# A three-part feed-forward/attention block in fp32: bursts of row maxima kept single, turned tiles in two banks, first loads on two queues

## The chip, the cores and the metric

One NeuronCore of a Trainium2 chip runs the whole kernel. The metric is the device time of one execution in microseconds (us); the median of three executions is compared. Besides those times there is one profiled execution, whose trace gives each instruction's start and length on each engine: TensorE (PE, with its weight loads PEld), VectorE (DVE), ScalarE (ACT), GpSimd (POOL), and SyncE (SP), which issues most DMAs.

## The reference

The input x has 4 sequences of 1024 tokens with 256 features, all in fp32. Three steps are added to it in turn: half a gated feed-forward layer of its layer norm, causal attention of its layer norm (16 heads of 16 features, with a rotation of q and k), and the same half feed-forward layer again.

```python
x = x + 0.5 * ffn(layernorm(x))          # silu(g) * u, 704 hidden
x = x + attn(layernorm(x))               # causal softmax, 16 heads of 16
x = x + 0.5 * ffn(layernorm(x))
# ffn:  g = (x @ gate_w.T) * gate_s ; u = (x @ up_w.T) * up_s
#       out = ((silu(g) * u) @ down_w.T) * down_s
# attn: att = softmax(q k^T / 4 + mask) ; out = (att v) @ Wo.T
```

## The kernel before

**Tiling.** The 4096 tokens are cut into eight blocks of 512, two to a sequence. For each block the kernel runs a first feed-forward layer (`ffn(i, 1)`), the projections (`qkv`), the attention, and a second feed-forward layer (`ffn(i, 2)`). Tokens of a block lie in four tiles of 128.

**Norm and turning.** `norm` makes statistics (VectorE, L364 and L367), a power on GpSimd (L373, L374) and the scaled tile (L386 on ScalarE, L382 on VectorE). The normed tile must have features on partitions. For most blocks that is done by VectorE's 32x32 transposes (L423) and a round trip through DRAM (`spread`, L433 and L439). For the first block's first layer, the first block's projections and the last block's second layer there is `turned` instead: four TensorE transposes of two tiles into one PSUM bank, and two copies out of it, one by ScalarE and one by VectorE (L456). In the very first layer, products of the identity with itself (`idle`, L411) stand ahead of the turns and ahead of the first gate product.

**Feed-forward.** Eleven products of 512 columns, two instructions each (L510), go into PSUM banks; ScalarE takes tanh (L524, L544), VectorE makes the gated hidden tile hT (L547, L550, and L527, L530 for the half chunk), and four down products of six instructions each (L570) are added to x (L576).

**Attention.** Each batch of two head groups is handled in two passes over scores. The first pass computes scores by query (L783), VectorE adds the causal mask where needed (L808) and takes negated row maxima (L835, L818) into nm. TensorE turns nm (L863), ScalarE copies it out (L868), and DMAs write it as an additional row into qT (L873), so that the second pass's scores by key (L898) already have the maximum taken off. ScalarE takes exp of these (L907), GpSimd masks the diagonal (L919), and products with v (L943) follow. A "half" is one pair of heads of one unit of scores: it takes two banks. A burst is two halves at a time, each using two of the four row groups of the array, so four banks: two halves of maxima, two of exps, or one of each.

**What sets the order.** All work is put into one program order by `Planner`, which runs when the program is built, with costs written by hand. `burst()` says which two halves could go next (a half of maxima with one of exps where both can, otherwise two alike). `step` compares that burst with the best other operation. After a burst it waits for `GAP` (1.6 us of other TensorE work) before the next one, except that a second burst may follow at once while TensorE is in "row" mode and fewer than `VISIT` (2) have been made: that is the variable `more`. PSUM has eight banks: bursts take from all of them; other products ("d") have at most four at a time.

**Start.** `load_first` issues the four tiles of block 0's x on SP (L353). `consts` issues the small gus table on ScalarE's queue, then the weights on SP, builds identity and causal mask on GpSimd, and there scales gus (L309, L310), which tanh and hidden use. The x of block 1 (L344) is issued after them, then the projections' weights.

Of the kernel before, what the change touches and what calls it, by code (L numbers as in the profile page):

```python
# [17 lines left out]
P = 128  # L18
# [25 lines left out]
class Planner:  # L44
# [83 lines left out]

    def step(self, burst):
        b = burst()  # L130
        more = self.mode == "row" and self.visit < self.VISIT
        due = b is not None and (more or self.since >= self.GAP)
        best = None
        for eng in self.ENGINES:
            for c in self.candidates(eng):
                s = max(c[0], self.busy["pe"] + 0.05) if eng == "pe" else c[0]
                if c[2].mode == "col" and self.mode == "full" and self.busy["pe"] < self.ready(c[2]) + self.PATIENCE:
                    s += self.HOLD
                if eng == "pe" and due and any(k.slot is None and k.kind == "d" for k in c[2].takes):
                    s += self.DUE  # L140
                key = (s, c[1])
                if best is None or key < best[0]:
                    best = (key, c)
        if b is not None:
            pe = self.busy["pe"]
            at = max(b[0], pe)
            if more:
                wait = self.SECOND
            else:
                wait = self.WAIT[self.mode]  # L150
                if self.since < self.GAP:
                    at += self.GAP - self.since
                elif self.since < self.LONG and b[2] is not None:
                    at = max(at, b[2] - 0.853 - 0.2 - self.SECOND)
            key = (max(at, pe + 0.05) - wait, 0)
            if best is None or key < best[0]:
                halves = b[1]
                us = max(h.us for h in halves) + 0.03 + (0.0 if self.mode == "row" else self.CHANGE["row"])
                at = max(b[0], pe, at if self.since >= self.GAP else 0.0)
                for h in halves:  # L160
                    h.us = us
                    self.place(h, at)
                self.visit = self.visit + 1 if self.mode == "row" else 1
                self.mode, self.since = "row", 0.0
                return b
        assert best is not None, "nothing can be placed"
        (s, _), (at, _, op, q) = best
        if op.eng == "pe":
            self.since += op.us
            if op.mode != self.mode:  # L170
                op.us += self.CHANGE[op.mode]
                self.mode = op.mode
        self.place(op, at)
        if q is not None:
            q.popleft()
        else:
            self.loose[op.eng].remove(op)
        return None
# [6 lines left out]
def dve_us(n):  # L185
    return n / 960 + 0.07


def act_us(n, ptr=0):
    return n / 1200 + 0.09 + 0.09 * ptr  # L190
# [3 lines left out]
def tile_macaron(  # L194
# [12 lines left out]
    nc = tc.nc  # L207
    B, T, D = x.shape
    I = wd.shape[0]
    H, HD, HP = 16, 16, 32  # L210
# [4 lines left out]
    BLK = 512  # L215
# [3 lines left out]
    NC = D // P  # L219
# [12 lines left out]
        xn=(4, [P, D]),  # L232
        xq=(2, [P, D]),
        xnT=(2, [P, NC, BLK]),
# [16 lines left out]
    for kind, (n, _) in shapes.items():  # L251
# [10 lines left out]
    ident = cpool.tile([P, P], F32, name="ident")  # L262
# [9 lines left out]
    plan = Planner(  # L272
        {k: v[0] for k, v in shapes.items()} | {k: len(v) for k, v in lasting.items()} | dict(d=dense, score=8),
        dict(d="bank", score="bank"),
    )
# [10 lines left out]
    xf_ = x.rearrange("b (k n p) d -> (b k) p n d", p=P, n=NB)  # L286
# [10 lines left out]
    def consts():  # L297
        nc.scalar.dma_start(out=gus_sb, in_=gus)
        w = wgu.rearrange("(c p) i -> p c i", p=P)
        for a, e in cuts:  # L300
            nc.sync.dma_start(out=wgu_sb[:, :, a:e], in_=w[:, :, a:e])
        nc.sync.dma_start(out=ds_sb, in_=ds.partition_broadcast(P))
        nc.sync.dma_start(out=wd_sb[:, :NF, :], in_=wd[: NF * P].rearrange("(c p) d -> p c d", p=P))
        nc.sync.dma_start(out=wd_sb[HALF:, NF, :], in_=wd[NF * P :])
        nc.gpsimd.memset(mhalf, -0.5)
        make_identity(nc, ident)
        make_causal_mask(nc, causal, mask_val=MASKED)

        nc.gpsimd.tensor_scalar(gus_sb[:, 0, :], gus_sb[:, 0, :], 0.5, None, ALU.mult)  # L309
        nc.gpsimd.tensor_tensor(gus_sb[:, 1, :], gus_sb[:, 1, :], gus_sb[:, 0, :], ALU.mult)  # L310

# [19 lines left out]
    filled = {k: [] for k in lasting}  # L331
# [2 lines left out]
    gu_loaded = Op("dma", 0.0, lambda: None)  # L334
    wd_loaded = Op("dma", 0.0, lambda: None)
    gu_loaded.done, wd_loaded.done = 7.5, 16.0
    wd_scaled = [Op("dve", 0.35, partial(scaled_wd, c), [wd_loaded], prio=4) for c in range(NI)]

    xb = [Buf("x") for _ in range(NBLK)]
    x0, x1, x2 = {}, {}, {}  # L340
# [9 lines left out]

    def load_first(j):
        def emit():
            nc.sync.dma_start(out=xb[0].tile[:, j, :], in_=xf_[0][:, j, :])  # L353

        x0[0, j] = Op("dma", 0.45, emit, takes=[xb[0]], tail=3.2)
        return x0[0, j]


# [49 lines left out]
    def idle(d, n):  # L408

        for _ in range(n):  # L410
            nc.tensor.matmul(d.tile[:, :P], ident, ident, start=True, stop=True)  # L411
# [31 lines left out]

    def turned(pair, j, xnT, prio, later, idles=0):

        d = Buf("d")

        def emit():
            idle(d, idles)
            for n, (xn, _) in enumerate(pair):  # L450
                for c in range(NC):
                    o = (c * 2 + n) * P
                    nc.tensor.transpose(d.tile[:, o : o + P], xn.tile[:, ts(c, P)], ident)

        def copy(c):
            (nc.vector.tensor_copy if c else nc.scalar.copy)(  # L456
                by_tile(xnT.tile[:, c])[:, j - 1 : j + 1],
                d.tile[:, ts(c, 2 * P)].rearrange("p (j a t) -> p j a t", j=2, t=HP),
            )

        t = Op("pe", 4 * 0.107, emit, [p[1] for p in pair], [d, xnT], [p[0] for p in pair], prio=prio)
        k = [Op("act", act_us(D), partial(copy, 0), [t], uses=[d, xnT], prio=later)]
        return t, [*k, Op("dve", dve_us(D), partial(copy, 1), [t], uses=[d, xnT], prio=later)]


    def ffn(i, which):
# [5 lines left out]
        xnT, xs = Buf("xnT"), Buf("xs")  # L472
        by_dma = (i, which) not in ((0, 1), (NBLK - 1, 2))
        very_first = (i, which) == (0, 1)
# [3 lines left out]
        for j in range(0, NB, 2):  # L478
            first, rest, pair = norm(i, j, src, 4, "xn")
# [17 lines left out]
            loose += squared + moves  # L497
        if very_first:

            for o in (f for k in filled.values() for f in k):  # L500
                o.deps += copies
        mids = []

        def product(d, cols, takes):
            for k in range(NC):

                def emit(k=k):
                    if very_first and cols.stop == 2 * I and not k:
                        idle(d, 2)
                    nc.tensor.matmul(  # L510
                        d.tile, wgu_sb[:, k, cols], by_tile(xnT.tile[:, k]), start=(k == 0), stop=(k == NC - 1)
                    )

                need = [*copies, gu_loaded]
                o = Op("pe", mm_us(BLK), emit, need, [] if k else takes, [d, xnT] if k else [xnT], prio=3)
                mids.append(o)
            return o
# [3 lines left out]
        d, a = Buf("d"), Buf("ta")  # L521
# [10 lines left out]
            )  # L532

        g = product(d, slice(2 * NF * P, 2 * I), [d, a, hT[NF]])
        t = Op("act", act_us(BLK, 1), tanh, [g], uses=[d, a], prio=2)
        v = Op("dve", dve_us(BLK), gated, [t], uses=[d, a], prio=2)
        h = Op("dve", dve_us(BLK), hidden, [v, *filled["hL"]], uses=[d, a, hT[NF]], prio=2)
        loose += [t, v, h]
# [233 lines left out]
    def max_half(blk, unit, pair, nm, reduces):  # L772
# [69 lines left out]

        for e in range(2):
            head(e)
        first.pair = pair
        return first

    def row_of_max(blk, g, nm, reduces):
# [38 lines left out]
    def exp_half(blk, unit, pair, pT, masks):  # L887
# [41 lines left out]
                last.append(Op("pool", 0.45, mask, done, uses=[pT], prio=0))  # L929
                loose_att.append(last[-1])  # L930
        masks.extend(last)
        first.pair = pair
        return first

    def weigh(blk, g, us, units, pTs, masks, av):
# [192 lines left out]
    with tc.manual_schedule():  # L1128
        for op in firsts:
            plan.place(op, plan.busy["dma"])  # L1130
        consts()
        plan.busy.update(dict.fromkeys(plan.busy, 3.5))
        plan.busy.update(act=5.0, dma=9.0)
        plan.place(loads.popleft(), 9.0)
        later()
        plan.busy.update(dma=20.0)
        plan.add(*wd_scaled, *(o for f in filled.values() for o in f))
        while True:
            next_ffn()
            pending = maxes or exps or todo  # L1140
            if not pending and not any(plan.loose.values()) and not any(any(q.values()) for q in plan.queues.values()):
                break
            b = plan.step(burst)
            if b is not None:
                for h in b[1]:
                    (maxes if maxes and h is maxes[0] else exps).popleft()
# [65 lines left out]
```

## Time and profile before

| | |
|---|---|
| median of 3 executions | 1060.93 us (1059.57 to 1061.2) |
| profiled execution | 1061.41 us, span of its instructions 1059.5 us |
| mean granted TensorE clock | 0.998 |
| TensorE busy | 1045.2 us (99%), 6546 records |
| VectorE busy | 807.8 us (76%) |
| ScalarE busy | 431.3 us (41%) |
| GpSimd busy | 295.0 us (28%) |
| DMA | 40.38 MB, mean 38 GB/s |

The span runs from the first to the last instruction; the execution's time has a little around it. In the timelines below, the columns are the start and the length in us, engine, line, operation, what it writes and reads, and how many records are merged; in brackets stand the idle time before it and what ended that. In windows, the columns are the stretch, its length, busy time (and records) of PE, PEld, DVE, ACT and POOL, the granted clock, the DMA share and GB/s. Matmul records overlap in the pipeline, so starts are a better measure than lengths.

### The profile page before, as it was taken

Reading aid. Unit: us, or ns where it says so; the run is one execution under the profiler, and the core shown is the slowest. Engines: PE = TensorE matmul, PEld = TensorE weight load, DVE = VectorE, ACT = ScalarE, POOL = GpSimd, SP = SyncE. Lnnn points to the kernel's source line nnn. Section 1 sums busy time; section 2 is a strip of 40 time slices with the busy share of each in tenths; the row PEclk is TensorE's granted clock in tenths of the full one; section 3 lists DMA queues with packets and bytes.
Section 4 is the critical chain, followed back from the end, with each engine's and each line's share of the span. In section 5 each row is a group of like instructions: output and inputs, shape, how many; then the busy total and the mean of one; then the engine's idle time right before and its main releaser. Section 6 shows DMA issues by size and latency. Waiting matters only on the chain.

```text
span 1059.5 us, 17448 instructions
## 1 busy us (share of the span) xinstructions
PE 1045.2 (99%) x6546; PEld 535.3 (51%) x6546; DVE 807.8 (76%) x1874; ACT 431.3 (41%) x821; POOL 295.0 (28%) x503
## 2 busy tenths in 40 slices
PE   8999999999999999999999999999999999999998
PEld 5645555454454464454544554463635644535465
DVE  6678989878898598778787898678798887783342
ACT  3213444345424444435343454444353454354421
POOL 5222431423111744212114432421215321122200
PEclk9999999999999999999999999999999999999999
DMA  8210210210202102100110102101021010010000
GB/s 288 57 41 2 71 31 7 65 31 4 71 8 61 41 2 51 32 30 31 51 51 11 31 13 59 31 22 40 2 61 41 11 51 2 11 51 12 11 20 20
DMA packets 43139, 40.38 MB, mean 38 GB/s; under 512 B 3952, under 2 KB 35760, under 8 KB 42928
## 3 DMA queue, kind: packets, MB, share of 16 engines
q1 hardware_dynamic: 42912, 39.27, 13.7%
q8 instruction: 51, 0.84, 0.3%
q14 instruction: 32, 0.26, 0.1%
q10 hardware_dynamic: 144, 0.01, 0.0%
HBM read 19.60 MB, written 15.20 MB: 33 GB/s over the span
## 4 chain that ended last, share of the span: by engine, by line
PE 90%; DVE 7%; DMA 1%; issue 1%; ACT 1%; SPq 1%; POOL 0%; DVEq 0%; ACTq 0%; POOLq 0%
PE bank L510 26%; PE bank L783 16%; PE bank L570 16%; PE bank L943 12%; PE bank L898 9%; PE bank L643 5%; PE bank L682 3%; PE bank L1015 2%; DVE nm L835 2%; DVE bank L808 1%; DMA x<-in_x 1%; DVE nm L818 1%; DVE hT L550 1%; DVE xs L423 0%; PE bank L863 0%
## 5 line engine op out<-in xcount | busy, mean ns | idle before, releaser
L907 ACT ACTIVATE pT<-bank 128x512 f32<-128x512 f32 x576 | 298.4, 601 | 305.3 <-PE bank L898 304.8
L835 DVE TENSOR_REDUCE nm<-bank 128x1 f32<-128x512 f32 (+2 forms) x640 | 330.6, 575 | 18.2 <-PE bank L898 17.0
L510 PE MATMUL bank<-xnT,wgu_sb 128*128 128x512 f32 x704 | 322.0, 601 | 1.6 <-DVE nm L835 0.7
L898 PE MATMUL bank<-qT,kT 17*128 17x512 f32 (+3 forms) x1536 | 287.0, 515 | 0.0
L783 PE MATMUL bank<-kT,qT 16*128 16x512 f32 (+3 forms) x1536 | 284.3, 508 | 2.5 <-DVE hT L550 1.7
L510 PEld LDWEIGHTS bank<-xnT,wgu_sb 128*128 128x128 f32 x704 | 127.0, 190 | 168.1 <-issue 112.5
L919 POOL TENSOR_SCALAR_AFFINE_SELECT pT<-pT 128x256 f32<-128x256 f32 x256 | 99.2, 407 | 393.6 <-ACT pT L907 393.4
L783 PEld LDWEIGHTS bank<-kT,qT 16*128 16x128 f32 x1536 | 110.8, 184 | 133.2 <-issue 35.9
L570 PE MATMUL bank<-wd_sb,hT 128*128 128x256 f32 x640 | 151.1, 382 | 1.1 <-DVE hT L550 1.1
L943 PE MATMUL bank<-pT,va 128*32 128x512 f32 (+3 forms) x1536 | 137.1, 490 | 1.4 <-DVE nm L835 1.3
L570 PEld LDWEIGHTS bank<-wd_sb,hT 128*128 128x128 f32 x640 | 122.2, 192 | 19.6 <-issue 1.5
L808 DVE TENSOR_TENSOR bank<-bank,causal 128x256 f32<-128x256 f32 (+1 forms) x320 | 104.2, 372 | 33.1 <-PE bank L898 28.8
L898 PEld LDWEIGHTS bank<-qT,kT 17*128 17x128 f32 x1536 | 109.7, 184 | 10.4 <-issue 3.6
L544 ACT ACTIVATE ta<-bank,gus_sb 128x512 f32<-128x512 f32 x80 | 54.9, 686 | 124.7 <-PE bank L510 124.4
L943 PEld LDWEIGHTS bank<-pT,va 128*32 128x32 f32 x1536 | 44.3, 109 | 96.4 <-issue 65.1
L547 DVE SCALAR_TENSOR_TENSOR ta<-ta,bank 128x512 f32<-128x512 f32 x80 | 54.8, 685 | 47.3 <-ACT ta L544 46.6
L975 POOL TENSOR_TENSOR oq<-oq 128x512 f32<-128x512 f32 x32 | 40.5, 1267 | 113.8 <-DVE oq L972 93.9
L550 DVE SCALAR_TENSOR_TENSOR hT<-bank,gus_sb,ta 128x512 f32<-128x512 f32 x80 | 59.5, 744 | 15.4 <-PE bank L510 14.1
L972 DVE STREAM_TRANSPOSE oq<-bank 128x512 f32<-128x512 f32 x64 | 45.5, 712 | 31.9 <-PE bank L943 31.6
L576 DVE TENSOR_TENSOR x<-bank,x 128x256 f32<-128x256 f32 x64 | 26.7, 417 | 55.8 <-PE bank L570 55.6
L643 PE MATMUL bank<-xnT,wqkv_sb 128*128 128x512 f32 x128 | 59.8, 602 | 0.1
L654 POOL TENSOR_TENSOR qs<-qs,rope_sb 128x512 f32<-128x512 f32 x32 | 40.6, 1271 | 45.3 <-DVE qs L651 45.0
(60 smaller groups left out, 671.5 us busy)
## 6 DMA issues: line engine op xcount, KB each, us to landing
xd<-xs SPq DMA_DIRECT2D x84, 128.0 KB
xnT<-xd SPq DMA_DIRECT2D x21, 512.0 KB
kT<-qT SPq DMA_DIRECT2D x64, 64.0 KB
out<-x SPq DMA_DIRECT2D x16, 256.0 KB
x<-in_x SPq DMA_DIRECT2D x7, 512.0 KB
qT<-nmT SPq DMA_DIRECT2D x128, 2.0 KB
wgu_sb<-in_wgu SPq DMA_DIRECT2D x2, 512.0 KB
rope_sb<-in_rope SPq DMA_DIRECT2D x1, 1024.0 KB
```

The costliest lines, as they stand in the source:

```text
L510: nc.tensor.matmul(d.tile, wgu_sb[:, k, cols], by_tile(xnT.tile[:, k]), start=(k == 0), stop=(k == NC - 1))
L544: nc.scalar.activation(a.tile, d.tile, AF.Tanh, scale=gus_sb[:, 0, c : c + 1])
L550: nc.vector.scalar_tensor_tensor(hT[c].tile, e.tile, gus_sb[:, 1, c : c + 1], a.tile, ALU.mult, ALU.mult)
L570: nc.tensor.matmul(d.tile[:, :D], hT[c].tile[:, ts(j, P)], wd_sb[:, c, :], start=(n == 0), stop=(n == NI - 1))
L643: nc.tensor.matmul(d.tile, wqkv_sb[:, k, ts(g, P)], xnT.tile[:, k, :], start=(k == 0), stop=(k == NC - 1))
L783: nc.tensor.matmul(sc[e].tile[:, c0 : c0 + w], qT[blk].tile[r, g, ts(j, P)], kt.tile[r, g, :w], start=True, stop=True,)
L808: nc.vector.tensor_tensor(d, d, causal.unsqueeze(1).to_broadcast([P, len(masked), P]), ALU.add)
L835: nc.vector.tensor_reduce(nm.tile[:, o : o + 1], sc[e].tile[:, c0 : c0 + w], AX.X, ALU.max, negate=True)
L898: nc.tensor.matmul(sc[e].tile[:, c0 : c0 + w], kt.tile[r, g, ts(k % NB, P)], qT[blk].tile[r, g, BLK - w :], start=True, stop=True,)
L907: nc.scalar.activation(pT.tile[:, e, :w], sc[e].tile[:, :w], AF.Exp)
L919: nc.gpsimd.affine_select(out=d, in_=d, compare_op=ALU.is_ge, fill=0.0, base=0, pattern=[[0, 2], [1, P]], channel_multiplier=-1,)
L943: nc.tensor.matmul(av.tile[ts(r, HP), BLK - w :], va[base + k // NB].tile[:, k % NB, h * VS : h * VS + HP], pTs[u, r // 2].tile[:, r % 2, ...
```

## The change

It has five parts.

1. `step`: `more` is also required not to be a burst of two halves of maxima. Such a burst now waits for the gap even right after another burst. To tell, each half carries a `kind`.
2. `turned` takes two banks; both tiles' first feature halves go to one, the second halves to the other. ScalarE copies one bank, VectorE the other.
3. The two idle products ahead of the first gate product are dropped (those ahead of the turns stay).
4. `load_first` issues tiles 2 and 3 on ScalarE's queue.
5. The scaling of gus becomes an operation of its own on GpSimd (`gus_scaled`), placed after the first layer's copies; the half chunk's tanh depends on it.

```diff
@@ step
-        more = self.mode == "row" and self.visit < self.VISIT
+        more = self.mode == "row" and self.visit < self.VISIT and b is not None and {h.kind for h in b[1]} != {"max"}
@@ consts
         make_causal_mask(nc, causal, mask_val=MASKED)
+    def scaled_gus():
         nc.gpsimd.tensor_scalar(gus_sb[:, 0, :], gus_sb[:, 0, :], 0.5, None, ALU.mult)
         nc.gpsimd.tensor_tensor(gus_sb[:, 1, :], gus_sb[:, 1, :], gus_sb[:, 0, :], ALU.mult)
...
+    gus_scaled = Op("pool", 0.5, scaled_gus, prio=6)
@@ load_first
-            nc.sync.dma_start(out=xb[0].tile[:, j, :], in_=xf_[0][:, j, :])
-        x0[0, j] = Op("dma", 0.45, emit, takes=[xb[0]], tail=3.2)
+            (nc.sync if j < 2 else nc.scalar).dma_start(out=xb[0].tile[:, j, :], in_=xf_[0][:, j, :])
+        x0[0, j] = Op("dma", 0.3, emit, takes=[xb[0]], tail=3.2)
@@ turned
-        d = Buf("d")
+        ds = [Buf("d") for _ in range(NC)]
         def emit():
-            idle(d, idles)
-            for n, (xn, _) in enumerate(pair):
-                for c in range(NC):
-                    o = (c * 2 + n) * P
-                    nc.tensor.transpose(d.tile[:, o : o + P], xn.tile[:, ts(c, P)], ident)
+            idle(ds[0], idles)
+            for c, d in enumerate(ds):
+                for n, (xn, _) in enumerate(pair):
+                    nc.tensor.transpose(d.tile[:, ts(n, P)], xn.tile[:, ts(c, P)], ident)
         def copy(c):
             (nc.vector.tensor_copy if c else nc.scalar.copy)(
                 by_tile(xnT.tile[:, c])[:, j - 1 : j + 1],
-                d.tile[:, ts(c, 2 * P)].rearrange("p (j a t) -> p j a t", j=2, t=HP),
+                ds[c].tile[:, : 2 * P].rearrange("p (j a t) -> p j a t", j=2, t=HP),
             )
@@ ffn
-            for o in (f for k in filled.values() for f in k):
+            for o in (gus_scaled, *(f for k in filled.values() for f in k)):
                 o.deps += copies
...
-                    if very_first and cols.stop == 2 * I and not k:
-                        idle(d, 2)
...
-        t = Op("act", act_us(BLK, 1), tanh, [g], uses=[d, a], prio=2)
+        t = Op("act", act_us(BLK, 1), tanh, [g, gus_scaled], uses=[d, a], prio=2)
@@ max_half / exp_half
-        first.pair = pair
+        first.pair, first.kind = pair, "max"      # "exp" in exp_half
```

More of the change, by code (lines that the diff above doesn't have):

```diff
@@ L457, in copy @@
                 by_tile(xnT.tile[:, c])[:, j - 1 : j + 1],
-                d.tile[:, ts(c, 2 * P)].rearrange("p (j a t) -> p j a t", j=2, t=HP),
+                ds[c].tile[:, : 2 * P].rearrange("p (j a t) -> p j a t", j=2, t=HP),
             )
-        t = Op("pe", 4 * 0.107, emit, [p[1] for p in pair], [d, xnT], [p[0] for p in pair], prio=prio)
-        k = [Op("act", act_us(D), partial(copy, 0), [t], uses=[d, xnT], prio=later)]
-        return t, [*k, Op("dve", dve_us(D), partial(copy, 1), [t], uses=[d, xnT], prio=later)]
+        t = Op("pe", 4 * 0.107, emit, [p[1] for p in pair], [*ds, xnT], [p[0] for p in pair], prio=prio)
+        k = [Op("act", act_us(D), partial(copy, 0), [t], uses=[ds[0], xnT], prio=later)]
+        return t, [*k, Op("dve", dve_us(D), partial(copy, 1), [t], uses=[ds[1], xnT], prio=later)]
     def ffn(i, which):
@@ L931, in exp_half @@
         masks.extend(last)
-        first.pair = pair
+        first.pair, first.kind = pair, "exp"
         return first
@@ L1136, in tile_macaron @@
         plan.busy.update(dma=20.0)
-        plan.add(*wd_scaled, *(o for f in filled.values() for o in f))
+        plan.add(gus_scaled, *wd_scaled, *(o for f in filled.values() for o in f))
         while True:
```

## The prediction

> **What bounds the kernel now.** I read the page's chain of waits first, then TensorE's timeline where that chain leaves TensorE, then VectorE's timeline there.
>
> ```profile
> PE 90%; DVE 7%; DMA 1%; issue 1%; ACT 1%; SPq 1%; POOL 0%; DVEq 0%; ACTq 0%; POOLq 0%
> ```
>
> TensorE ends the program; the 7% of VectorE are places where TensorE stood still for it. Back to back, a record of 128x512 starts every 0.429 us (L510: 16 in 7.03), one of 128x256 every 0.216; an fp32 product is two records. Four row groups share the array in L783 and L898, so one burst (16 records, or 8 long ones) is worth 0.86 us. TensorE's timeline around the costliest place:
>
> ```profile
> 60.76 1.14 PE L783 MATMUL bank<-kT,qT 16*128 16x512 f32 x8
> 61.83 6.28 PE L510 MATMUL bank<-xnT,wgu_sb 128*128 128x512 f32 x14
> 68.03 2.17 PE L783 MATMUL bank<-kT,qT 16*128 16x128 f32 x32
> 70.68 3.70 PE L510 MATMUL bank<-xnT,wgu_sb 128*128 128x512 f32 x8 [0.47 <-DVE nm L835]
> 74.64 1.89 PE L570 MATMUL bank<-wd_sb,hT 128*128 128x256 f32 x8
> 77.14 0.30 PE L863 MATMUL bank<-ident,nm 128*128 128x128 f32 x1 [0.60 <-DVE nm L818]
> 78.50 0.70 PE L570 MATMUL bank<-wd_sb,hT 128*128 128x256 f32 x2 [1.07 <-DVE hT L550]
> 79.04 0.97 PE L570 MATMUL bank<-wd_sb,hL 128*128 128x256 f32 x2
> 79.80 3.25 PE L570 MATMUL bank<-wd_sb,hT 128*128 128x256 f32 x8
> 82.98 0.70 PE L783 MATMUL bank<-kT,qT 16*128 16x512 f32 x2
> ```
>
> A lone burst of maxima takes 61.83-60.76 = 1.07. The doubled one at 68.03 takes 2.65, and its eight banks then hold VectorE:
>
> ```profile
> 69.20 0.76 DVE L808 TENSOR_TENSOR bank<-bank,causal 128x256 f32<-128x256 f32 x2 [0.31 <-PE bank L783]
> 71.86 1.41 DVE L835 TENSOR_REDUCE nm<-bank 128x1 f32<-128x384 f32 x4
> 75.71 1.28 DVE L818 TENSOR_REDUCE nm<-bank 128x2 f32<-128x512 f32 x2
> 76.91 0.68 DVE L547 SCALAR_TENSOR_TENSOR ta<-ta,bank 128x512 f32<-128x512 f32 x1
> 77.70 0.75 DVE L550 SCALAR_TENSOR_TENSOR hT<-bank,gus_sb,ta 128x512 f32<-128x512 f32 x1
> ```
>
> From 69.20 to 76.9 VectorE does nothing but that visit; the turn of the row maxima (L863) and hT (L550), which the down product needs, come behind it. The idle time then costs a second time. The windows view (PEclk after the busy columns):
>
> ```profile
> 79.10:82.50 3.40, 3.40 (x10) 2.69 (x9) 1.03 (x3) 0.00 (x0) 0.00 (x0) 0.50 0.01 2
> 84.00:86.00 2.00, 2.00 (x13) 1.75 (x10) 1.86 (x5) 1.09 (x2) 0.42 (x1) 1.00 0.00 0
> ```
>
> Another doubled visit, at 154.57, is worse still (2.74):
>
> ```profile
> 154.57 2.12 PE L783 MATMUL bank<-kT,qT 16*128 16x128 f32 x32
> 157.31 2.14 PE L943 MATMUL bank<-pT,va 128*32 128x512 f32 x24 [0.62 <-DVE nm L835]
> ```
>
> And the start:
>
> ```profile
> 9.21 0.71 PE L411 MATMUL bank<-ident 128*128 128x128 f32 x4 [0.92 <-ACT xnT L456]
> 16.00 0.43 DVE L364 BATCH_NORM_STATS2 st<-x 128x6 f32<-128x256 f32 x1 [1.19 <-DMA x<-in_x]
> 16.34 0.73 DVE L550 SCALAR_TENSOR_TENSOR hT<-bank,gus_sb,ta 128x512 f32<-128x512 f32 x1
> 17.13 7.13 PE L510 MATMUL bank<-xnT,wgu_sb 128*128 128x512 f32 x16 [0.34 <-DVE hT L550]
> ```
>
> The second group of gate products waits at 17.13 for hT, which stands behind the first statistics of block 1, whose x lands at 15.97.
>
> **What the Trainium skill says.** "TensorE: Matmul & The Clock Gate", Part 1, puts a granted clock of one half after an idle window of about 3.4 us; the trace agrees in size (clock 0.50 for 3.4 us), although TensorE had not been idle for all of the stretch before. "PSUM — Partial Sum Buffer", the section on bank collisions, forbids two engines one bank at a time and lets ScalarE and VectorE read different banks together: ScalarE's copy (L456) starts at 7.76 and 8.79, each time after VectorE's of the same bank (7.30 and 8.33, 0.42 long). "DMA: Bandwidth & Descriptors", Issuing engines are not separate DMA queues, says that a second issuing engine saves issue time alone; the windows of 6 to 8 us show a DMA share of 1.00 to 1.07, so bandwidth is scarce there.
>
> **The change part by part.** Where instructions move I read from the order of both programs. On TensorE the last 1806 of 3303 instructions are the same in both; in the trace of before these begin at about 494.8 us. VectorE's last 911 and ScalarE's last 444 agree too. So only the start and the first 495 us can differ; the tail with the last turned tiles is alike in order, and TensorE doesn't wait for those copies at 1014 to 1017.
>
> Start. Without two idle products (L508) and with copies side by side, the first gate product waits for copies that end at about 8.75 instead of 9.16, and 0.43 of idle products go: it comes at 8.9 instead of 9.76. The two loads moved to ScalarE's queue take 0.43 us of issue each from SP, so all behind them (gate and up weights, wd, x of block 1) is issued 0.87 earlier. But x's first four tiles now share the engines two by two: the first pair, for which the statistics waited until 3.11, may land up to 0.5 later, the second, waited for until 4.44, some 0.4 earlier, so the norm chain moves by -0.3 to +0.25; I take 0. ScalarE has nothing in 0 to 3.1 that the issue could delay; the gus scaling on POOL comes behind the norms but ahead of the memsets of kT, and 3 us ahead of the first tanh (11.68). None of this reaches the end by itself: VectorE's order is unchanged there, so the second group still starts 1.16 us after x of block 1 lands. Its issue moves by 0.87, but its landing hangs on the transfers ahead of it: the DMA share is 0.73 in 3 to 4 us and 0.72 in 5 to 6, where earlier issues find room (0.5 together), and 1.00 or more in 6 to 8. I take -0.5 (bounds -1.1, the issue with some spread, and +0.2).
>
> Turned tiles of qkv(0): the copies at 46.78 and 47.20 become parallel; TensorE's L643 starts at 47.62 where 47.35 was due. -0.3 (0 to -0.3).
>
> First block's maxima. In the new order the two bursts of 68.03 stand apart: one, then 4 products of L510 and 6 of L570, the next, 12 products of L570, a third, then the turn. VectorE needs 73.2-69.2 = 4.0 us for a burst and some 2.9 for two ta/hT pairs; TensorE gives it 1.07+0.2+3.43+2.59 = 7.3. Before the turn it has 5.2+1.07+0.2 = 6.4 against 3.7 plus about 1.2 of adds and statistics. So these waits go: 77.14-(74.64+8x0.216) = 0.77, 78.50-(77.14+0.107) = 1.25, and with no idle stretch the half clock, 82.98-79.04-10x0.216 = 1.78. Sum -3.8. Next late there is hT of the last chunk, due within 0.1 of its use: 0 to 0.3 given back.
>
> Row visits in the first 495 us. Excess of a visit over 0.86 a burst, from its first start to the next product: lone maxima 0.21; the five doubled ones 0.93, 1.02, 0.46, 1.01, 0.21 (sum 3.6); 56 mixed doubles 0.34 in the mean (19.2), five odd ones 1.2 together. Before: 67 visits, 24.2. After: 8 lone maxima and 61 mixed doubles, 8x0.21+61x0.343 = 22.6. -1.6. Stretches of full-array products fall from 57 to 55, and each costs 0.2 to enter (61.83 to 68.03 is 6.20 for 14x0.429 = 6.01): -0.4.
>
> Other waits for VectorE in that part: 0.48 (the turn at 167.15), 0.34 (295.67), 0.45 (before 317.53), 0.3 (near 327) and 0.2 (348), 1.8 in all, mostly soon after doubled or four-exp visits. The new order has mixed doubles only, as the kept half has; that half shows 0.2, 0.43, 0.2 and 0.38 in 565 us, so by length 1.0 remains. -0.8 (bounds -1.5 and +2).
>
> Sum: -0.5-0.3-3.8-1.6-0.4-0.8 = -7.4. The profiled execution took 1061.41 with a span of 1059.5; that becomes a span of 1052.1 and 1054.0. The median of before is 0.5 below the profiled one: 1053.5.
>
> **Rivals.** (A) The gap at 68 to 83 us goes, but the new order brings as many waits elsewhere as it removes: for it speaks that all later visits are re-dealt; against it that they are the kind which the kept half shows. -0.5-0.3-3.8 = -4.6: 1056.3. (B) More gain: x of block 1 lands over a microsecond sooner and the redealt part shows no waits: -1.1-0.3-3.8-1.6-0.4-1.8 = -9.0: 1051.9 and below. (C) The start gives nothing and the turn at 77 keeps half its wait and the half clock: -0.3-1.9-1.6-0.4 = -4.2+1.0 = -3.2: 1057.7. (D) Slower: the turns of the row maxima, now nearer to the bursts that feed them. The new second turn stands only four L510 (3.6 us) behind two mixed bursts with 128 and 384 columns, for which VectorE needs 2.1 each; four turns before 495 us have 4.1 to 4.9 us. Should each wait 0.8 to 0.9 and trip the half clock as at 79 us (1.8), each costs 2.6, four cost 10.6: 1053.5+10.6 = 1064.1. It decides from three such turns on. Against it: turns at the same distance in the kept half waited at most 0.43 and never tripped the clock (PEclk 1.00 from 82.5 us on).
>
> **How the numbers follow.** Forecast 0.62, A 0.17, B 0.08, C 0.06, D 0.07. The forecast alone spans 1052 to 1055.8 (its terms' bounds, not all at one end); with A, B and a part of C the range is 1051 to 1057.5. No change that can be told is within 0.2%, 1058.8 to 1063.05: only the edges of C and D lie there, 0.05. Faster 0.89, slower 0.06.
>
> **What would show it.** A granted clock of 1.00 from 8 us to the end but for the last microseconds; the first gate product near 8.9 and the second group where x of block 1 lands plus 1.16; the turn (L863 before) without a wait near 77 to 80; no visit of maxima above 1.1 us; the kept half as long as before, within 0.3. The forecast is wrong if the half clock comes back at any place, if the kept half changes length, or if x of block 1 lands later than at 16.

## The result and the profile after

The changed kernel takes 1055.71 us in the median of six executions (1055.34 to 1057.61), against 1060.78 us (1059.57 to 1061.34) for the kernel before on the same chip: a ratio of 0.9959, 95% interval 0.9946 to 0.9972. The forecast was 1053.5 us, range 1051.0 to 1057.5. The profiled execution of the changed kernel took 1055.71 us, with a span of 1053.8 us against 1059.5.

The chain of waits on the page (shares by engine) has less of VectorE in it: 4% instead of 7%.

```profile
PE 93%; DVE 4%; DMA 1%; ACT 1%; issue 0%; SPq 0%; DVEq 0%; ACTq 0%
```

TensorE's timeline at the place of the doubled burst (some lines between these are left out; lines of the kernel have moved, so that L784 here is L783 before):

```profile
67.82 1.16 PE L784 MATMUL bank<-kT,qT 16*128 16x128 f32 x16
68.91 3.70 PE L511 MATMUL bank<-xnT,wgu_sb 128*128 128x512 f32 x8
75.20 1.16 PE L784 MATMUL bank<-kT,qT 16*128 16x256 f32 x16
81.66 1.14 PE L784 MATMUL bank<-kT,qT 16*128 16x512 f32 x8
82.73 0.33 PE L864 MATMUL bank<-ident,nm 128*128 128x128 f32 x1
82.90 0.60 PE L571 MATMUL bank<-wd_sb,hL 128*128 128x256 f32 x2
```

Every burst of maxima is alone (eight in the trace, none longer than 1.09 us; the first here goes from 67.82 to 68.91), and the turn of the row maxima (L864) has no bracket: it waits for nothing. The windows view of the same kernel shows the granted clock (1.00, third column from the right) where it was 0.50:

```profile
79.10:82.50 3.40, 3.40 (x21) 2.28 (x19) 2.55 (x7) 0.00 (x0) 0.93 (x2) 1.00 0.00 0
```

The start is another matter. From TensorE's timeline and VectorE's:

```profile
8.98 7.10 PE L511 MATMUL bank<-xnT,wgu_sb 128*128 128x512 f32 x16 [0.56 <-ACT xnT L459]
17.28 1.13 PE L511 MATMUL bank<-xnT,wgu_sb 128*128 128x512 f32 x2 [1.20 <-DVE hT L551]
...
16.15 0.43 DVE L368 BATCH_NORM_STATS2 st<-x 128x6 f32<-128x256 f32 x1 [2.05 <-DMA x<-in_x]
```

The first gate product comes at 8.98 instead of 9.76, and all of that is lost again: the second group waits 1.20 us, not 0.34, because the x of block 1 lands no earlier: at 16.12 us instead of 15.97. It was not issued earlier either. With two loads on the other queue SP comes to its first weight load at 1.70 instead of 2.67, but then takes longer over the weights' issues, and comes to this load 0.38 later than before (SP's timeline, first before, then after):

```profile
6.60 1.72 SPq L344 DMA_DIRECT2D x<-in_x  x1
6.98 0.58 SPq L348 DMA_DIRECT2D x<-in_x  x1
```

To see where time goes I compare the traces at equal work: TensorE's products are added up at their back-to-back prices, and the time at which each kernel reaches a given sum is set against the other. A second trace of the kernel before (run e11 below, without a half clock) is the better partner, and the table uses it.

| work done (us) | changed minus before (us) | what lies there |
|---|---|---|
| 6 | -0.39 | first gate products earlier (-0.39 here; the partner's were earlier than in the first trace) |
| 10 | +0.32 | x of block 1 |
| 45 | -0.05 | copies of the projections' turned tiles |
| 60 to 70 | -0.74 to -2.88 | the doubled burst and the waits behind it |
| 85 to 100 | -2.75 to -1.63 | given back |
| 170 | -4.55 | doubled bursts at 154 and 165 us gone |
| 450 | -4.23 | orders are equal from here on |
| 940 | -3.97 | the end |

Between 60 and 450, where the two orders differ, a single value wobbles by up to some 0.5 with the products that happen to stand there; the other values are firm.

### The profile page after: what moved, and what is told of

Read it like the earlier page. It is cut to its first block, busy times and chain, and to the rows that moved or that the text cites. A ratio compares the mean times of both kernels' runs of the same rounds, so it can differ in the third digit from the quotient of the medians.

```text
span 1053.8 us, 17435 instructions
## 1 busy us (share of the span) xinstructions
PE 1042.0 (99%) x6542; PEld 534.2 (51%) x6542; DVE 807.8 (77%) x1874; ACT 430.4 (41%) x821; POOL 295.7 (28%) x503
## 4 chain that ended last, share of the span: by engine, by line
PE 93%; DVE 4%; DMA 1%; ACT 1%; issue 0%; SPq 0%; DVEq 0%; ACTq 0%
PE bank L511 27%; PE bank L784 16%; PE bank L571 16%; PE bank L944 12%; PE bank L899 10%; PE bank L644 5%; PE bank L683 3%; PE bank L1016 3%; DMA x<-in_x 1%; DVE nm L836 1%; DVE bank L809 1%; PE bank L864 0%; DVE hT L551 0%; DVE nm L819 0%; ACT pT L908 0%
## 5 line engine op out<-in xcount | busy, mean ns | idle before, releaser
L784 PE MATMUL bank<-kT,qT 16*128 16x512 f32 (+3 forms) x1536 | 289.6, 508 | 1.9 <-DVE hT L551 1.5
L899 PE MATMUL bank<-qT,kT 17*128 17x512 f32 (+3 forms) x1536 | 291.0, 514 | 0.0
L784 PEld LDWEIGHTS bank<-kT,qT 16*128 16x128 f32 x1536 | 112.5, 184 | 133.0 <-issue 33.9
```

The source lines that it names most:

```text
L784: nc.tensor.matmul(sc[e].tile[:, c0 : c0 + w], qT[blk].tile[r, g, ts(j, P)], kt.tile[r, g, :w], start=True, stop=True,)
L899: nc.tensor.matmul(sc[e].tile[:, c0 : c0 + w], kt.tile[r, g, ts(k % NB, P)], qT[blk].tile[r, g, BLK - w :], start=True, stop=True,)
```

## The experiments

Nine kernels were run, one of them twice, and the kernel before twice more for its trace. "Before" times are of the same chip in the same batch.

**The rule alone, and everything but the rule.** e1 is the kernel before with the rule; its compute order is that of the changed kernel but for the turned tiles and the two idle products.

```diff
-        more = self.mode == "row" and self.visit < self.VISIT
+        more = self.mode == "row" and self.visit < self.VISIT and b is not None and {h.kind for h in b[1]} != {"max"}
```

> The kernel before with the rule for bursts of maxima alone (one bank for turned tiles, idle products and one load queue as before). My theory: the rule carries the gain, by taking away VectorE's backlog at 68 to 78 us and the half clock after it; only the 0.37 us of the qkv copies is missing, so about 1056.1 us, 4.7 below the kernel before, with a granted clock of 1.00 at 79 us. Rival: the start's parts are worth a microsecond or more of the 5.1; then 1057 or above.

Measured: 1055.26 us (1054.82 to 1057.28), ratio to before 0.9956 (0.9944 to 0.9968). The rule alone is as good as the whole change; it was expected a little behind it (1056.1) and lies 0.45 below its median, which the spread of both covers.

e2 is the reverse: the changed kernel with that line as it was.

> The changed kernel with the old rule (all start parts kept). My theory: the first gate product is near 9.0 us, but the second group of gate products waits for x of block 1 as before (17.1 to 17.3), so only the qkv copies' 0.37 is left: 1060.3 to 1060.6 us, and the stall at 76 to 78 us with the half clock is back. Rival: the start gives 1 us or more: 1059.7 or below.

Measured: 1059.56 us (13 executions, 1058.8 to 1061.43) against 1060.26; ratio 0.9994 (0.9986 to 1.0002). The median lies in the rival's window, but the interval allows no change at all. In its trace block 1's x was there at 15.47, by luck (see e4), so TensorE gained 0.53 there and 0.37 at the qkv copies. The start's parts are worth between nothing and 1.5 us by that interval, and these times don't tell more.

**What the start waits for.** In e3 the load of block 1's x is issued ahead of ds and wd.

```diff
             nc.sync.dma_start(out=wgu_sb[:, :, a:e], in_=w[:, :, a:e])
+        plan.place(loads.popleft(), 9.0)
         nc.sync.dma_start(out=ds_sb, in_=ds.partition_broadcast(P))
...
-        plan.place(loads.popleft(), 9.0)
         later()
```

> The changed kernel with the load of block 1's x issued on SP ahead of ds and wd instead of behind them; the order on all compute engines is the same. My theory: the wait at 16 us for that x eats the start's gain; with it gone VectorE's statistics and hT run 1.2 to 1.4 us earlier and all behind moves along: 1054.3 to 1054.6 us, second gate group at about 15.9. Rival: wd, now later, becomes the wait (down products start at 24.5), or the gain is lost further on: 1055.4 or above.

VectorE's timeline has no wait for x any more, and hT (L552) runs 2 us earlier than in the changed kernel:

```profile
14.04 0.42 DVE L369 BATCH_NORM_STATS2 st<-x 128x6 f32<-128x256 f32 x1
14.44 0.75 DVE L552 SCALAR_TENSOR_TENSOR hT<-bank,gus_sb,ta 128x512 f32<-128x512 f32 x1
```

At a work of 10 us this kernel is 1.43 us ahead of the changed one, and 1.51 at the end of the program: the gain lasts, and wd is not missed. The span was 1052.3 us. The times say less: 1056.19 us in the median, which is in the rival's window (1055.4 or above), with three executions at 1054.1 to 1055.4 and three at 1057.0 to 1057.5. Of these three slower ones, two have a full granted clock (1.0), so what made them slow stays open. The trace (of a 1054.2 execution) supports the theory; the median does not. e8 below shows the same step without the scatter.

e4 puts all four first loads back on SP.

```diff
-            (nc.sync if j < 2 else nc.scalar).dma_start(out=xb[0].tile[:, j, :], in_=xf_[0][:, j, :])
+            nc.sync.dma_start(out=xb[0].tile[:, j, :], in_=xf_[0][:, j, :])
```

> The changed kernel with all four first loads on SP again; compute order the same. My theory: the transfers are bound by the DMA engines, so the second queue moves x of block 1 by nothing that helps: within 0.3 us of the changed kernel (1055.4 to 1056.0), x of block 1 again near 16.0, the first statistics at 3.1 instead of 3.5. Rival: the second queue does help and without it x lands 0.5 or more later: 1056.2 or above.

Measured: 1055.25 us (1054.48 to 1056.76), 0.15 below the expected window and 0.46 below the changed kernel's median, which the spread of both covers. Block 1's statistics started at 16.35. Over the twelve traces with that load in its old place they started at 14.89 to 16.35, with two queues (16.15, 15.47, 15.21, 14.89, 15.70, 15.95) as with one (16.00, 15.70, 16.35, 15.44, 15.83, 15.17); at 15.21 x was already there. The load itself was issued at 6.77 in the mean with two queues and at 6.58 with one: from the first weight load to this one SP took 5.06 instead of 3.92 us, so the 0.96 that it was ahead was lost again. Why the issues take longer was not tested. So the second queue moves nothing that can be seen here.

**VectorE's backlog.** e5 is the kernel before, e6 the changed kernel, both without the mask additions of the first pass. The maximum is then taken over later keys too; the second pass keeps its mask, and the order of all other instructions is unchanged.

```diff
-                    nc.vector.tensor_tensor(d, d, causal.unsqueeze(1).to_broadcast([P, len(masked), P]), ALU.add)
+                    del d
```

> The kernel before without the 320 mask additions of VectorE on the scores of the first pass (L808): the maximum is then taken over later keys too, and the second pass keeps its mask; order of all else unchanged. My theory: the doubled bursts cost time only through VectorE's backlog. That at 69 to 77 us shrinks by 2.8 us, so the waits of 0.77 and 1.25 go, and with them the half clock (1.78); with shorter waits elsewhere 1054 to 1055.5 us. Rival: the loss at 68 to 83 us lies in the doubled visit itself or in the clock, whatever VectorE has to do: 1058 or above, half clock still at 79 us.

> The changed kernel without the same mask additions (L809), order unchanged. My theory: what was lost between 93 and 115 us (1.2 us) and the waits left near 163, 292, 311 and 344 us are VectorE's, which is 97% busy there; so 1052.5 to 1053.5 us, and the distance to the kernel before without mask additions shrinks from 5 to 2 or less. Rival: those losses are of TensorE's own order (more visits, more entries): 1055 or above and the distance stays at 5.

Measured: 1052.12 us and 1051.37 us, against 1059.86 (ratios 0.9923, interval 0.9911 to 0.9935, and 0.9914, interval 0.9901 to 0.9927). Both gained more than was expected; by equal work some 2 us of each gain lie behind 450 us, in the part that the change leaves alone. TensorE's timeline of e5 around the doubled burst:

```profile
67.48 2.17 PE L783 MATMUL bank<-kT,qT 16*128 16x128 f32 x32
69.58 3.70 PE L510 MATMUL bank<-xnT,wgu_sb 128*128 128x512 f32 x8
73.55 1.89 PE L570 MATMUL bank<-wd_sb,hT 128*128 128x256 f32 x8
75.27 0.27 PE L863 MATMUL bank<-ident,nm 128*128 128x128 f32 x1
75.38 0.61 PE L570 MATMUL bank<-wd_sb,hT 128*128 128x256 f32 x2
```

The burst is still doubled, and takes 2.10 instead of 2.65; the turn and the down product wait for nothing. With less work on VectorE the two kernels lie 0.75 us apart instead of 5.1. The doubled burst by itself costs next to nothing; what it costs is VectorE's queue behind it. Between 85 and 100 us of work e6 gains 0.43 on the changed kernel, which lost 1.1 there, so the masks are a part of that loss and not all of it.

**Which bursts matter.** In e7 the rule holds for block 0 alone, in e9 for all blocks but block 0.

```diff
-        first.pair, first.kind = pair, "max"
+        first.pair, first.kind = pair, "max" if blk == 0 else "late"     # e7
+        first.pair, first.kind = pair, "max" if blk else "early"         # e9
```

> The changed kernel with the rule only for the maxima of block 0; later double bursts of maxima are allowed again (one remains in the order, beside a few lone bursts). My theory: the gain is that of the first place, so this stays within 0.7 of the changed kernel: 1055.2 to 1056.4 us. Rival: the later doubled bursts and the re-dealing after them matter as much as my sum put them (1.6 for visits and 0.8 for waits): 1056.8 to 1058.

> The changed kernel with the rule for the maxima of all blocks but block 0, so the doubled burst at 68 us is back and the later ones are gone. My theory: the loss at 68 to 83 us (waits 2.0 and the half clock's 1.8) is back, the rest of the gain stays: 1058.0 to 1059.5 us, with a half clock near 79 us. Rival: without the later doubled bursts nothing is left to gain once the first is back, or all is: 1060 or above, or 1057 or below.

Both theories failed, and e9's time lies in its rival's window (1057 or below). e7 took 1059.9 us (14 executions, 1057.19 to 1061.98; ratio 0.9998, 0.9989 to 1.0007): no gain in the median. e9 took 1055.48 us (1054.84 to 1056.85; ratio 0.9961, 0.9947 to 0.9975): all of it. Yet e9 has the doubled burst, and both waits:

```profile
67.37 2.17 PE L784 MATMUL bank<-kT,qT 16*128 16x128 f32 x32
76.47 0.30 PE L864 MATMUL bank<-ident,nm 128*128 128x128 f32 x1 [0.60 <-DVE nm L819]
77.84 0.70 PE L571 MATMUL bank<-wd_sb,hT 128*128 128x256 f32 x2 [1.07 <-DVE hT L551]
```

and, in the windows view, no half clock behind them:

```profile
76.00:78.00 2.00, 0.46 (x2) 0.30 (x3) 1.67 (x3) 0.25 (x1) 0.00 (x0) 1.00 0.00 0
78.40:81.80 3.40, 3.40 (x20) 2.10 (x18) 1.05 (x4) 0.00 (x0) 0.00 (x0) 1.00 0.01 2
```

At equal work e9 is 0.50 ahead of the kernel before at 70 us, where the changed kernel is 2.88 ahead; at 450 us they stand at 4.63 and 4.23. So what the lone bursts of block 0 save is given back. The traces show most of it: in e9 the visits' excess over 0.86 a burst (counted as in the prediction) is 20.8 and the other waits for VectorE are 1.05, in the changed kernel 21.7 and 1.73. Three visits of the changed kernel, at 90.7, 97.0 and 108.6 us, have an excess of 0.76, 0.52 and 0.52, where e9 has none above 0.45.

e10 ran e7's kernel once more for a second trace.

> The kernel with the rule for block 0 alone, once more, for a second trace: its executions lay between 1057.2 and 1062.0, and the trace shown was of the quickest. My theory: the slower ones carry one or two stretches of half clock that the quickest escaped, after TensorE's idle of over 1 us behind a doubled burst (near 165 us) or at the kept half's turn near 532 us; each costs about 1.7 us. Rival: the same waits are longer in slower executions, with the clock at 1.00 throughout.

It took 1058.25 us with the clock at 1.00 from 10 us on. The 1.06 between the two traces is all there at a work of 10 us: it is the landing of block 1's x. Both traces show a new wait, behind two lone bursts that now stand close together:

```profile
162.72 0.84 PE L784 MATMUL bank<-kT,qT 16*128 16x256 f32 x12
167.79 1.14 PE L784 MATMUL bank<-kT,qT 16*128 16x512 f32 x8 [1.44 <-DVE nm L819]
```

None of the longer executions of e7 was traced, but the granted clock of each is on record: 0.999 in its four quickest (1057.2 to 1058.4 us), 0.998 or 0.995 in the other ten (1059.1 to 1062.0). That speaks for the half clock, as expected for e10; at which waits it came is not shown. Against executions of the kernel before with a clock of 0.999 or more, those four are quicker by 1.5 in the median, so the rule in block 0 alone is not worth nothing in every execution; e7's trace was also helped by an early landing of block 1's x (14.89).

**The half clock.** e11 and e12 are the kernel before, traced again.

> The kernel before once more, for a second trace. Its executions lie in two groups, near 1059.6 and near 1061.3 us; the one profiled first (1061.41) had the half clock at 79 us. My theory: the waits of 0.77 and 1.25 at 76 to 78 us are in every execution, but the half clock behind them only in the slower group; an execution near 1059.6 has the clock at 1.00 from 8 us to the end. Rival: the half clock at 79 us is in every execution, and the groups differ by something else (x of block 1, or another place).

> As the run before it, one more trace of the kernel before: whichever group it falls in, a time near 1061.3 should go with one stretch of half clock and a time near 1059.6 with none. Rival: time and half clock don't go together.

They took 1059.59 and 1058.95 us, both with the same two waits and without a half clock, as the theory said. The windows view of e11:

```profile
76.00:78.50 2.50, 0.83 (x4) 0.31 (x3) 2.16 (x4) 0.25 (x1) 0.00 (x0) 1.00 0.00 0
79.10:82.50 3.40, 3.40 (x19) 2.12 (x18) 1.23 (x5) 0.14 (x1) 0.00 (x0) 1.00 0.01 2
```

TensorE is as idle from 76 to 78.5 as in the first trace (0.83 of 2.50 busy in both), and then runs 19 records in 3.4 us where the first trace had 10. e1's trace shows the opposite case: an order that the changed kernel shares, and a half clock where the changed kernel's trace has none.

```profile
532.50:535.90 3.40, 3.40 (x5) 1.34 (x6) 2.77 (x8) 1.34 (x4) 0.62 (x1) 0.51 0.01 2
```

Over the work from 450 to 600 us e1 lost 1.68 by it. That execution took 1056.81 us; four of e1's six took 1054.8 to 1055.4. Before, e1 and e2 each had one profiled execution with such a stretch (1061.41, 1056.81, 1060.51), all in the upper part of their kernel's times.

The granted clock of every execution says the same of the kernel before. Of its 48 executions beside the experiments, 32 had a clock of 0.999 or 1.0 and took 1058.99 to 1060.42 us; 16 had 0.998 and took 1060.86 to 1062.98. The changed kernel is not free of it: one of its six had 0.997 (1057.61), though its trace shows a full clock until the last microseconds. And it does not explain every slow execution: another of the changed kernel's (1057.45) and two of e3's had a clock of 1.0.

**Together.** e8 joins e3's earlier load and e6's missing additions.

> The changed kernel with block 1's x issued ahead of ds and wd, and without the mask additions on the first pass's scores. My theory: the two gains are of different stages and add: 1.2 to 1.4 below the changed kernel without mask additions, 1051.2 to 1052.3 us, and the half clock that some executions show near 532 us no longer occurs, since the turn's wait there is gone, so the executions lie within 1 us of each other. Rival: they overlap, 1052.5 or above, or two groups of times 1.5 to 2 us apart remain.

Measured: 1050.18 us (1050.12 to 1051.39), 1.19 below e6, ratio to before 0.9907 (0.9893 to 0.9921), the best of all. By equal work the earlier load is worth 1.27 here, where e3's trace had 1.5, so the two gains add. Its four executions lie within 1.3 us, not 1, and the time is 1.0 below the expected window, as e6's was; no half clock is in its trace before the last microsecond.

## Why the prediction was right, and where it was not

The direction, the part of the change that carries the gain (the rule) and the range were right; the size was not, nor the place of the gain: -7.4 us forecast, -5.1 measured (-5.7 between the two profiled executions, -3.9 between spans without a half clock, 1057.7 and 1053.8). The time lies at the edge of what the forecast's own terms spanned (1055.8). In number rival A, with its chance of 0.17, was nearer (1056.3); that too is in part luck, since A counts the start and the half clock in full.

- **Start (-0.5 forecast).** Two of its statements held: the first product came near 8.9 (8.98), and the second group 1.16 after x of block 1 lands (16.12 plus 1.16 is 17.28). The wrong term is the issue of that load: it was to move by -0.87 and moved by +0.38, since SP's issues of the weights took longer. The landing moved by +0.15 and not -0.5. A landing later than 16 us was one of the prediction's own signs of being wrong. e4 shows no effect of the second queue beyond a scatter of 1.5.
- **Projections' turned tiles (-0.3).** -0.37.
- **First block's maxima (-3.8): the step that failed.** The waits of 0.77 and 1.25 went, as said, and nothing new took their place next to them. But 1.78 of the sum was the half clock, taken as certain because the one trace showed it. e11 and e12 show that the waits don't bring it every time. And the 2.0 that remain do not reach the end: with the waits left in (e9) the kernel is as quick. The sum allowed 0 to 0.3 to be given back; the traces show 1.1 at 85 to 100 us of work, and the rest later.
- **Row visits (-1.6).** Counted the same way between 20 us and the common part, the excess over 0.86 a burst fell from 24.2 to 21.7: -2.5. The visits came out as counted (8 lone and 61 mixed), but the mixed ones became a little cheaper (0.33 in the mean), which the sum held constant at 0.343. This term came out larger than forecast and hid a part of the others' shortfall.
- **Entries into full-array stretches (-0.4).** 56 became 54 after 20 us, but the small excesses of those products, waits left aside, stayed at some 11.5 us in all: nothing.
- **Other waits (-0.8).** The largest failure of kind after the clock: 1.8 before, 1.7 after. The doubled bursts' waits went, and new ones of 0.2 to 0.4 came near 165, 293, 312, 345 and 350 us. The kept half of the program was no guide to the re-dealt half.

That the kept half would keep its length held (564.7 and 565.0 us). Rival D, new waits at the row maxima's turns, did not come: the turns after 82 us waited at most 0.43 (in its sum, four times 2.6 is 10.4 and not 10.6). Of rival A this much was true: the gain at 68 to 83 us is partly returned, by 1.1 us at 85 to 100 us of work, where VectorE is the bound. The windows view of that stretch (VectorE's busy time of 30 us is the third after the comma), first for e11, then for the changed kernel:

```profile
85.00:115.00 30.00, 30.00 (x180) 14.62 (x182) 28.83 (x79) 15.10 (x28) 7.95 (x19) 1.00 0.13 36
85.00:115.00 30.00, 29.76 (x182) 13.93 (x181) 29.08 (x78) 15.01 (x28) 7.47 (x18) 1.00 0.14 37
```

VectorE is busy for 28.83 and 29.08 of 30, in either kernel nearly all the time; only in the changed kernel does TensorE stand still (0.24). A plausible reading is a debt: maxima that were not done early are done there. e5 and e6 support it (without 320 additions the two orders end 0.75 apart), but that the debt is exactly what e9 spares was not tested by itself.

## What to carry to other kernels

Ask of a removed wait whether the engine that was waited for has spare time afterwards: where it is 97% busy, the saved time can be lost again, as that of block 0 was here, and less work on that engine may give more than a better order (the additions left out gave 7.7 us, the change 5.1). Before an earlier start counts as a gain, look for the next thing that has a fixed time of its own, here one load, and look when it is issued as well as when it lands. And before pricing a clock event take a second trace, and read the granted clock of every execution: one trace shows one toss.

## What the runs showed of the hardware

TensorE's half clock for 3.4 us came behind idle stretches, but not each time: the doubled burst with the same two waits (0.77 and 1.25 us) was followed by it in two traces (the kernel before at 79 us, e2 at 78) and not in three (e9, e11, e12), and the kept half's wait of 0.43 near 532 us was followed by it in one trace (e1) and not in that of the changed kernel. In neither place did TensorE stand still for 3.4 us. The Trainium skill ("TensorE: Matmul & The Clock Gate", Part 1) says that the window of activity runs freely and isn't tied to the program; the traces agree with that, though no run here moved the window by itself. Each of the two events whose cost was read took 1.7 to 1.8 us. In the kernel before that is most of the distance between its lower and its upper times; in others a part of that distance has another cause, which stays open.
